# Four small edits at the joints of an attention kernel: value pieces at other steps, last sums in PSUM, half a norm on ScalarE

## The chip, the cores and the metric

The kernel runs on one core of a Trainium2 chip. The metric is the device time of one execution, in microseconds; a comparison takes the median of several runs. A core has five engines, each with its own queue of instructions, executed in order: PE (TensorE, matrix products, which it writes to the eight banks of PSUM), DVE (VectorE), ACT (ScalarE), POOL (GpSimd) and SP, which only starts transfers. They wait for each other by semaphores.

## What is computed

A chain of four blocks on x of shape 8 x 256 x 32 x 32, in float32: an attention block with an MLP, a deformable convolution, a binary convolution and another deformable convolution. The change lies in the first block, which is, cut to what matters:

```python
h = bn(x, g1, b1)                       # x as (8, 256, 1024), normed over batch and pixels
q, k, v = wq @ h + bq, wk @ h + bk, wv @ h + bv      # 16 heads; q, k of 16 rows, v of 64
a = softmax(q^T k * scale, axis=-1)     # 1024 x 1024 for each image and head
x = x + wp @ (a @ v) + bp
h = bn(x, g2, b2)
x = x + w2 @ relu6(w1 @ h + bb1) + bb2
```

## The kernel before, in words

**Tiling of attention.** The 8 images times 4 groups of 4 heads are 32 *groups* (b, g). A group has two *blocks* (b, g, h), h being a half (512) of the queries, so there are 64 blocks. A block goes over the 1024 keys in NT = 8 chunks of 128, one chunk to a *step*; there are 512 steps, 16 to a group. Of a step t:

- `exps` computes the scores of step t + 1 on PE (L453, four matmuls, keys on partitions) and their exponentials on ScalarE (L454). The maximum over the keys has been put into q as a row of its own, so that the matmul subtracts it.
- `attend` multiplies the exponentials of step t with the values on PE (L465), and sums exponentials over chunks by element: `esum`, L473 for the first two chunks, L475 for the others, on GpSimd; for the second pair of heads of the last block on VectorE.
- `score_max` finds the maxima for a later block (AHEAD = NT + 3 = 11 steps ahead): scores in bf16 pieces on PE (L408), maxima on VectorE (L412). `found(0)` to `found(3)` are four such pairs within a step. The first block has no bf16 pieces yet and takes `score_max_first` (L421 and L424), four pairs in each of the steps -11 to -4, which are the ramp; `enter_max` (L430 to L441) then turns the maxima and puts them into q with four small transfers.

**Order.** On PE, ScalarE, VectorE and GpSimd the order of instructions is the order of these calls, written out by hand (`manual_schedule`); SP's order is left to a scheduler. Work beside the core of the loop is entered by `plan(step, place, f, ...)`: in each step, the places 0, 1 and 2 run after `found(2)` and before `found(3)`.

**What is planned, for group n = (b, g) beginning at step t0:** the four pieces of the next group's values (`project_v`, eight matmuls and a copy by ScalarE to a piece, L391 and L395) at steps 0, 1, 2, and the fourth at 4 for even n and at 9 for odd n; the first group's own four pieces at -9, -7, -5 and -3; q and k of the next pair of groups (`project_qk`, L333) at 8, 9, 10 and 14 of even n, with their division into bf16 levels (`split`, L359 and L366 on VectorE, L364 on ScalarE) at 9 to 18; the transfers of the levels (`stack`, L374) and of q and k (`spread`, L380). A block's sums are taken by PE with a matrix of ones (`totals`, L486) three steps after its end, inverted and laid out by transfers, and its outputs scaled on GpSimd (L518) and projected (`add_projected`, L548) some steps later. The values of images after the first are normed on ScalarE (L317).

**The end.** The last block has a shorter way, `total_last` with reciprocals straight from PSUM (L526), and `scale_last` (L539, L540). Then follow `add_projected` (L548 on PE, L556 and L558 on VectorE), the batch norm's scale and shift (`batch_norm`, L207 to L219), and the MLP, which begins with `normed` (L749, two halves `t` of 128 channels) and `hidden` (L775). The MLP, the convolutions and the sampling between them are put in order by a planner with fixed costs (`Order`); the change doesn't touch its costs.

**Buffers that matter.** `bank()` in attention takes one of two PSUM banks (`pb`), shared by maxima, values, q and k, totals and projections; the scores have four (`sc`), the products with the values two. Exponentials have six tiles (`e`), two to a step. GpSimd and VectorE are the only engines that release them, except that the products on PE must be done too.

Of the kernel before, what the change touches and what calls it, by code (L numbers as in the profile page):

```python
# [12 lines left out]
AF = mybir.ActivationFunctionType  # L13
ALU = mybir.AluOpType
# [4 lines left out]
P = 128  # L19
# [4 lines left out]
NT = N // P  # L24
# [134 lines left out]
def conv_seq_kernel(ctx: ExitStack, tc: tile.TileContext, d: dict, out: bass.AP):  # L159
    nc = tc.nc  # L160
# [6 lines left out]
    x = const.tile([P, 2, B, N], F32, name="x")  # L167
# [12 lines left out]
    def col(name, i=0, n=1, p=P):  # L180
        o = COL[name] + i
        return vec[:p, o : o + n]
# [52 lines left out]
    wide = const.tile([P, 2, HID], F32, name="wide")  # L235
    with ExitStack() as s0:
# [20 lines left out]
        ones = w.tile([P, HD], F32, name="ones_a")  # L257
# [15 lines left out]
        for dst, name, eng in ((wq, "wqT", nc.sync), (wk, "wkT", nc.scalar)):  # L273
            padded = ep.tile([P, 2, HALF], F32, name="e")
            eng.dma_start(padded, d[name].rearrange("(t p) o -> p t o", p=P))
            for t in range(2):
                src = padded[:, t, :].rearrange("p (n r) -> p n r", r=32)[:, :, 0:KD]
# [3 lines left out]
        for dst, name, scale in ((bq4, "bq", 4.0), (bk, "bk", 1.0)):  # L281
            ps = ps_p.tile([P, 512], F32, name="pb")
            for c in range(4):
                nc.tensor.matmul(
                    ps[c % 2 * 64 : c % 2 * 64 + 64, c // 2 : c // 2 + 1], taken.rearrange("p n r -> p (n r)"), col(name, c),
                    start=True, stop=True,
# [8 lines left out]
        def bank():  # L295
            return ps_p.tile([P, 512], F32, name="pb")
# [11 lines left out]
        ys, vss, outs = {}, {}, {}  # L308

        def normed(b, t, h):  # L310
            if t == h == 0:
                ys[b] = yp.tile([P, 2, N], F32, name="y")
            cols = slice(h * HALF, (h + 1) * HALF)
            if b == 0:
                nc.vector.tensor_scalar(ys[b][:, t, cols], x[:, t, b, cols], s1[:, t : t + 1], t1[:, t : t + 1], ALU.mult, ALU.add)
            else:
                nc.scalar.activation(ys[b][:, t, cols], x[:, t, b, cols], AF.Identity, bias=t1[:, t : t + 1], scale=s1[:, t : t + 1])  # L317
# [34 lines left out]
        def split(b, g2, i, stage):  # L352

            which, h = QK[i]
            u, rest, lev = parts[i]

            eng = nc.gpsimd if (b, g2) == (0, 0) else nc.vector
            if stage == 0:
                eng.tensor_sub(rest, u, lev[0])  # L359
                return  # L360
            if lev[stage] is None:
                lev[stage] = lp.tile([P, HALF], BF16, name="lev")
            if stage == 1:
                nc.scalar.copy(lev[1], rest)  # L364
            else:
                eng.tensor_sub(lev[2], rest, lev[1])  # L366
            nc.sync.dma_start(lev_d[b, g2][which, stage, :, h * HALF : (h + 1) * HALF], lev[stage])
# [14 lines left out]
        def project_v(b, g, i):  # L382

            if i == 0:
                vss[b, g] = vp.tile([P, NT, 256], F32, name="v")
            ps = bank()
            for mt in (2 * i, 2 * i + 1):
                for t in range(2):
                    for c in range(2):
                        k0 = mt * P + c * 64  # L390
                        nc.tensor.matmul(  # L391
                            ps[c * 64 : (c + 1) * 64, (mt % 2) * 256 : (mt % 2 + 1) * 256], ys[b][:, t, k0 : k0 + 64],
                            wv[:, t, g * 256 : (g + 1) * 256], start=t == 0, stop=t == 1,
                        )
            nc.scalar.copy(vss[b, g][:, 2 * i : 2 * i + 2, :], ps.rearrange("p (m c) -> p m c", c=256))  # L395
# [47 lines left out]
        es = {}  # L443
# [12 lines left out]
        avs, sums = {}, {}  # L456

        def attend(m, kt, pair):
            b, g, h = m
            if kt == 0:  # L460
                avs[m, pair] = ps_v.tile([P, HALF], F32, name="av")
            av, e = avs[m, pair], es[m, kt, pair]
            for i in range(2):
                j = 2 * pair + i
                nc.tensor.matmul(  # L465
                    av[i * HD : (i + 1) * HD, :], vss[b, g][:, kt, j * HD : (j + 1) * HD], e[:, i, :],
                    start=kt == 0, stop=kt == NT - 1,
                )

            eng = nc.vector if m == blocks[-1] and pair else nc.gpsimd  # L470
            if kt == 1:
                sums[m, pair] = ap.tile([P, 2, HALF], F32, name="esum")
                eng.tensor_add(sums[m, pair], es.pop((m, 0, pair)), es.pop((m, 1, pair)))  # L473
            elif kt > 1:
                eng.tensor_add(sums[m, pair], sums[m, pair], es.pop((m, kt, pair)))  # L475
            if kt == NT - 1:
                outs[m, pair] = op.tile([P, HALF], F32, name="o")
                nc.scalar.copy(outs[m, pair], avs.pop((m, pair)))
# [3 lines left out]
        def totals(m):  # L482

            ps = bank()
            for j in range(4):
                nc.tensor.matmul(ps[32 * j : 32 * j + 32, :], ones[:, 0:32], sums[m, j // 2][:, j % 2, :], start=True, stop=True)  # L486
            return ps

        def total(m):
# [71 lines left out]
        blocks = [(b, g, h) for b, g in groups for h in range(2)]  # L561
# [7 lines left out]
        def plan(step, place, f, *args):  # L569
            work.setdefault((step, place), []).append(lambda: f(*args))  # L570

        for n, (b, g) in enumerate(groups):
            t0 = n * 2 * NT
            nxt = groups[n + 1] if n + 1 < len(groups) else None
            if nxt:
                for i in range(4):
                    plan(t0 + (0, 1, 2, 9 if n % 2 else 4)[i], 1, project_v, *nxt, i)
                    plan(t0 + 9 + i, 0, spread, *nxt, i)
                for pair in range(2):
                    for i in range(8):  # L580
                        plan(t0 + (1, 1, 2, 2, 2, 3, 3, 3)[i] + 4 * pair, 2, stack, *nxt, pair, i)
                if nxt == groups[-1]:
                    plan(t0 + 8, 2, nc.sync.dma_start, wide, d["w1T"].rearrange("(t p) o -> p t o", p=P))
            if g == 2 and b + 1 < B:
                for i in range(4):
                    plan(t0 + 5 + i // 2, i % 2, normed, b + 1, i // 2, i % 2)
            if n % 2 == 0 and n + 2 < len(groups):
                b_, g2 = groups[n + 2][0], groups[n + 2][1] // 2

                for i in range(4):  # L590
                    plan(t0 + (8, 9, 10, 14)[i], 1, project_qk, b_, g2, i)
                    at = t0 + (9, 11, 14, 17)[i]
                    plan(at, 0, split, b_, g2, i, 0)
                    plan(at, 2, split, b_, g2, i, 1)
                    plan(t0 + (10, 12, 16, 18)[i], 0, split, b_, g2, i, 2)
        for n, m in enumerate(blocks):
            b, g, h = m
# [43 lines left out]
        with tc.manual_schedule(engines={mybir.EngineType.PE, mybir.EngineType.Activation, mybir.EngineType.DVE, mybir.EngineType.Pool}):  # L641
            for t in range(2):
                for h in range(2):
                    normed(0, t, h)

            nc.scalar.dma_start(wv, d["wvT"].rearrange("(t p) o -> p t o", p=P))
            nc.gpsimd.dma_start(wp, d["wpT"].rearrange("(t p) o -> p t o", p=P))
            nc.gpsimd.dma_start(bv, d["bv"].rearrange("(t p) -> p t", p=P))
            for t in range(2):
                bias(t)  # L650
            for i in range(4):
                project_qk(0, 0, i)
                which, h = QK[i]
                for j in range(4):
                    dst = (qs, ks)[which][0][32 * j : 32 * j + KD, h * HALF : (h + 1) * HALF]
                    (nc.gpsimd if j % 2 else nc.sync).dma_start(dst, parts[i][0][j * KD : (j + 1) * KD, :])
                split(0, 0, i, 0)
            for i in range(4):
                plan(2 * i - 9, 1, project_v, 0, 0, i)
                split(0, 0, i, 1)  # L660
                split(0, 0, i, 2)
            for pair in range(2):
                for i in range(8):
                    stack(0, 0, pair, i, (nc.sync, nc.gpsimd))
            for t in range(-AHEAD, steps + 2 * NT):
                step(t)
            assert not work
# [11 lines left out]
    with ExitStack() as s1_:  # L679
# [34 lines left out]
        ones = w.tile([P, 1], F32, name="ones")  # L714
# [27 lines left out]
        ys, hids, pss = {}, {}, {}  # L742

        def normed(b, h):

            ys[b, h] = sb.tile([P, 2, HALF], F32, name="y")
            cols = slice(h * HALF, (h + 1) * HALF)
            for t in range(2):
                nc.vector.tensor_scalar(ys[b, h][:, t, :], x[:, t, b, cols], s2[:, t : t + 1], t2[:, t : t + 1], ALU.mult, ALU.add)  # L749

        def signs(t, i):

# [375 lines left out]
        b = B - 1  # L1128
# [21 lines left out]
        b = B - 1  # L1150
# [17 lines left out]
        with tc.manual_schedule(engines={mybir.EngineType.PE, mybir.EngineType.Activation, mybir.EngineType.DVE, mybir.EngineType.Pool}):  # L1168
            s2, t2 = batch_norm(1, col("g2", 0, 2), col("b2", 0, 2))
# [8 lines left out]
    with ExitStack() as s3_:  # L1178
# [61 lines left out]
        def bank3():  # L1240
# [17 lines left out]
            ps=2, pc=1, pd=1, pw=3, pa=1,  # L1258
# [374 lines left out]
        ps = bank3()  # L1633
# [247 lines left out]
```

## Time and profile before

| what | us |
|---|---|
| median of three runs (4491.49, 4504.40, 4504.44) | 4504.4 |
| the profiled execution | 4512.47 |
| its span, first to last instruction | 4510.7 |
| start to the first exponential's scores | 0 to 90.5 |
| attention from there to its last projection | 90.5 to 2661.5 |
| MLP, samples and binary convolution, first L775 to last L775 | 2667.2 to 3611.7 |

In a line of the timeline stand the start in us, the length in us (of a run of like instructions, where xN is over 1, from the first start to the last end), the engine, the line of the code, the operation, what it writes and reads, its sizes, and in brackets how long the engine had been idle before it and what ended that. A float32 matmul of the code is two in the trace, so the eight matmuls of a piece of values are x16. The windows give busy time by engine in a stretch of the span, with the mean granted clock of TensorE and the transfers.

### The profile page before, as it was taken

To read this page: it belongs to the slowest core of one execution; us is meant where nothing else is said; L and a number is where in the kernel's file an instruction comes from. 1 tells how busy PE (TensorE), PEld (TensorE's weight loads), DVE (VectorE), ACT (ScalarE), POOL (GpSimd) and SP (SyncE) were. 2 spreads that over 40 slices of the span, in tenths; PEclk is the share of its full clock that TensorE was granted. 3 is DMA by queue.
4 is the path that set the end of the run, shared out by engine and by line. 5 is a ranking of instruction groups with operands and counts; after the bars stand their busy time and mean duration, and the time that the engine had idled before them with its cause. 6 is when DMAs were issued, how large, how long until landed. Compare 5 with 4: busy or idle time off the path is not lost. (4 is left out here: it accounts for less than half of the span.)

```text
span 4510.7 us, 59867 instructions
## 1 busy us (share of the span) xinstructions
PE 4026.9 (89%) x20901; PEld 1530.0 (34%) x20901; DVE 2856.0 (63%) x4976; ACT 1875.1 (42%) x3366; POOL 3316.1 (74%) x2019
## 2 busy tenths in 40 slices
PE   6999999999999999999999998666767766899877
PEld 3333333333333333333333333222223322344332
DVE  5666666666666666666667653444445444688885
ACT  2555555555555555555555542211212111534331
POOL 3989988888888988898888954454454553078887
PEclk8999999999999999999999998888778878999978
DMA  5222221221222122122222112222232331100000
GB/s 164 67 63 56 63 75 57 63 69 57 61 72 63 56 64 74 56 61 70 59 62 71 48 45 69 78 80 79 76 96 68 89 110 60 40 10 15 15 15 24
DMA packets 224279, 284.12 MB, mean 63 GB/s; under 512 B 104400, under 2 KB 134624, under 8 KB 223712
## 3 DMA queue, kind: packets, MB, share of 16 engines
q1 hardware_dynamic: 193408, 196.49, 14.8%
q0 software_dynamic: 28720, 77.90, 5.8%
q10 hardware_dynamic: 1840, 5.81, 0.3%
q8 instruction: 168, 2.75, 0.3%
q14 instruction: 143, 1.17, 0.1%
HBM read 214.10 MB, written 64.34 MB: 62 GB/s over the span
## 5 line engine op out<-in xcount | busy, mean ns | idle before, releaser
L475 POOL TENSOR_TENSOR esum<-esum,e 128x1024 f32<-128x1024 f32 x762 | 1821.5, 2423 | 55.9 <-ACT e L454 55.4
L412 DVE TENSOR_REDUCE pm<-pb 128x1 f32<-128x512 f32 x2016 | 1372.9, 688 | 772.5 <-PE pb L408 769.7
L454 ACT ACTIVATE e<-sc 128x512 f32<-128x512 f32 x2048 | 1056.6, 603 | 601.0 <-PE sc L453 594.0
L465 PE MATMUL av<-e,v 128*64 128x512 f32 x4096 | 1048.5, 592 | 0.0
L930 POOL DMA_INDIRECT g<-table,idx x576 | 549.0, 953 | 583.4 <-DVE near_p L952 308.3
L408 PE MATMUL pb<-sk,sq 128*64 128x512 bf16 x4032 | 765.7, 386 | 17.8 <-DVE pm L412 17.1
L453 PE MATMUL sc<-q,k 32*128 32x512 f32 x4096 | 593.0, 639 | 0.0
L408 PEld LDWEIGHTS <-sq 128*64 128x64 bf16 x4032 | 247.2, 109 | 862.9 <-issue 849.1
L473 POOL TENSOR_TENSOR esum<-e 128x1024 f32<-128x1024 f32 x127 | 303.1, 2407 | 249.8 <-ACT e L454 246.5
L465 PEld LDWEIGHTS av<-e,v 128*64 128x64 f32 x4096 | 287.6, 137 | 232.1 <-issue 138.1
L788 PE MATMUL po<-hid,kept 128*128 128x512 f32 x512 | 260.1, 657 | 72.9 <-DVE x L792 56.4
L1500 POOL TENSOR_TENSOR part<-part,pr 128x512 f32<-128x512 f32 x212 | 275.8, 1301 | 55.4 <-DVE pr L1483 44.1
L1483 DVE TENSOR_TENSOR pr<-pw,v 128x512 f32<-128x512 f32 x394 | 253.8, 682 | 61.7 <-POOL part L1500 31.8
L1301 PE MATMUL pc<-xpad,kept 128*128 128x512 f32 x576 | 276.5, 604 | 11.2 <-DMA bom<-in_l_bom 7.9
L775 PE MATMUL pm<-y,wide 128*128 128x512 f32 x512 | 248.1, 632 | 17.0 <-ACT hid L780 11.3
L391 PE MATMUL pb<-wide,y 128*64 128x256 f32 x2048 | 248.6, 386 | 0.2 <-DVE pm L412 0.2
L453 PEld LDWEIGHTS sc<-q,k 32*128 32x128 f32 x4096 | 167.0, 183 | 231.0 <-issue 182.1
L548 PE MATMUL pb<-o,wp 128*64 128x512 f32 x1024 | 244.5, 598 | 0.4 <-DVE o L540 0.2
L780 ACT ACTIVATE hid<-pm,vec 128x512 f32<-128x512 f32 x128 | 86.8, 685 | 278.7 <-PE pm L775 142.5
L395 ACT COPY v<-pb 128x512 f32<-128x512 f32 x128 | 74.9, 585 | 296.1 <-PE pb L391 296.1
L952 DVE TENSOR_TENSOR near_p<-g,near_p 128x320 f32<-128x320 f32 (+1 forms) x384 | 177.3, 462 | 13.2
L391 PEld LDWEIGHTS pb<-wide,y 128*64 128x64 f32 x2048 | 143.5, 139 | 116.6 <-DVE pm L412 51.6
(266 smaller groups left out, 3927.2 us busy)
## 6 DMA issues: line engine op xcount, KB each, us to landing
sq<-lev_d SPq DMA_DIRECT2D x512, 64.0 KB
r<-inv_d SPq DMA_DIRECT2D x252, 128.0 KB
sk<-lev_d SPq DMA_DIRECT2D x496, 64.0 KB
lev_d<-lev SPq DMA_DIRECT2D x180, 128.0 KB
u_d<-u SPq DMA_DIRECT2D x60, 256.0 KB
g<-table,idx POOLq DMA_INDIRECT x576
out<-res SPq DMA_DIRECT2D x32, 256.0 KB
q<-u_d SPq DMA_DIRECT2D x124, 64.0 KB
```

The source lines that it names most:

```text
L391: nc.tensor.matmul(ps[c * 64 : (c + 1) * 64, (mt % 2) * 256 : (mt % 2 + 1) * 256], ys[b][:, t, k0 : k0 + 64], wv[:, t, g * 256 : (g + 1) * ...
L408: nc.tensor.matmul(ps[c * 64 : (c + 1) * 64, :], sq[pair][:, c, q0 : q0 + 64], sk[pair][:, c, kh * HALF : (kh + 1) * HALF], start=True, st ...
L412: nc.vector.tensor_reduce(maxima[m][:, pair, qt, kh : kh + 1], ps, AX.X, ALU.max)
L453: nc.tensor.matmul(ps, k[r, kt * P : (kt + 1) * P], q[r, h * HALF : (h + 1) * HALF], start=True, stop=True)
L454: nc.scalar.activation(es[m, kt, j // 2][:, j % 2, :], ps, AF.Exp)
L465: nc.tensor.matmul(av[i * HD : (i + 1) * HD, :], vss[b, g][:, kt, j * HD : (j + 1) * HD], e[:, i, :], start=kt == 0, stop=kt == NT - 1,)
L473: eng.tensor_add(sums[m, pair], es.pop((m, 0, pair)), es.pop((m, 1, pair)))
L475: eng.tensor_add(sums[m, pair], sums[m, pair], es.pop((m, kt, pair)))
L788: nc.tensor.matmul(pss["o", b, h, t], w2[:, j, t * P : (t + 1) * P], hids[b, h, j], start=j == 0, stop=j == 7)
L930: nc.gpsimd.indirect_dma_start(out=g[:, k, :], out_offset=None, in_=tables[b][:TR, :], in_offset=bass.IndirectOffsetOnAxis(ap=idxs[b][:, t ...
L1301: nc.tensor.matmul(S["c", b, h], wc[:, t, k, :], tap(xpads[t], k, H // 2, h * H // 2), start=t == k == 0, stop=t == 1 and k == 8,)
L1500: nc.gpsimd.tensor_add(S["part", b, h], S["part", b, h], S.pop(("pr", b, h, on_pool[n])))
```

## The change

Four things are edited.

1. `attend` doesn't add the exponentials of the last block's last two chunks; `totals` reads these tiles on PE instead and accumulates three sets of four matmuls in the bank, the sums last.
2. Steps of the values' pieces: the first group's pieces go from -9, -7, -5, -3 to one before the loop, then -3, -2 and 3; the fourth piece of the next group goes to step 12 in groups with g = 0 (it was at 4), and stays at 4 for g = 2 and at 9 for odd g.
3. The load of the MLP's first weights (`w1T`) is planned at step 13 of its group instead of 8.
4. In `normed` of the MLP, the second half of the first image's first pixels is computed by ScalarE instead of VectorE.

```diff
@@ attend @@
             eng = nc.vector if m == blocks[-1] and pair else nc.gpsimd
-            if kt == 1:
+            if m == blocks[-1] and kt > NT - 3:
+                pass
+            elif kt == 1:
                 sums[m, pair] = ap.tile([P, 2, HALF], F32, name="esum")
@@ totals @@
             ps = bank()
-            for j in range(4):
-                nc.tensor.matmul(ps[32 * j : 32 * j + 32, :], ones[:, 0:32], sums[m, j // 2][:, j % 2, :], start=True, stop=True)
+            late = (NT - 2, NT - 1) if m == blocks[-1] else ()
+            for i in range(len(late) + 1):
+                for j in range(4):
+                    src = es[m, late[i], j // 2] if i < len(late) else sums[m, j // 2]
+                    nc.tensor.matmul(
+                        ps[32 * j : 32 * j + 32, :], ones[:, 0:32], src[:, j % 2, :], start=i == 0, stop=i == len(late),
+                    )
             return ps
@@ the plan by groups @@
             if nxt:
+
+                late = {0: 12, 2: 4}.get(g, 9)
                 for i in range(4):
-                    plan(t0 + (0, 1, 2, 9 if n % 2 else 4)[i], 1, project_v, *nxt, i)
+                    plan(t0 + (0, 1, 2, late)[i], 1, project_v, *nxt, i)
                     plan(t0 + 9 + i, 0, spread, *nxt, i)
...
                 if nxt == groups[-1]:
-                    plan(t0 + 8, 2, nc.sync.dma_start, wide, d["w1T"].rearrange("(t p) o -> p t o", p=P))
+                    plan(t0 + 13, 2, nc.sync.dma_start, wide, d["w1T"].rearrange("(t p) o -> p t o", p=P))
@@ before the loop over steps @@
                 split(0, 0, i, 0)
+            project_v(0, 0, 0)
             for i in range(4):
-                plan(2 * i - 9, 1, project_v, 0, 0, i)
+                if i:
+                    plan((-3, -2, 3)[i - 1], 1, project_v, 0, 0, i)
                 split(0, 0, i, 1)
@@ normed of the MLP @@
             for t in range(2):
-                nc.vector.tensor_scalar(ys[b, h][:, t, :], x[:, t, b, cols], s2[:, t : t + 1], t2[:, t : t + 1], ALU.mult, ALU.add)
+                if b == h == 0 and t:
+
+                    nc.scalar.activation(ys[b, h][:, t, :], x[:, t, b, cols], AF.Identity, bias=t2[:, t : t + 1], scale=s2[:, t : t + 1])
+                else:
+                    nc.vector.tensor_scalar(ys[b, h][:, t, :], x[:, t, b, cols], s2[:, t : t + 1], t2[:, t : t + 1], ALU.mult, ALU.add)
```

## Prediction, written before the changed kernel ran

> **What bounds the kernel now.** I read the page first, then the windows over attention in stretches of 100 us, then the timelines of the four places that the diff touches: its ramp, the steps 11 to 13 of its groups, its end, and the first matmuls of the MLP.
>
> ```profile
> PE 4026.9 (89%) x20901; PEld 1530.0 (34%) x20901; DVE 2856.0 (63%) x4976; ACT 1875.1 (42%) x3366; POOL 3316.1 (74%) x2019
> ...
> PE   6999999999999999999999998666767766899877
> ```
>
> Attention is slices 2 to 23, and TensorE is full there: over 25 windows of 100 us (100 to 2600 us) PE is busy 2484.28 of 2500 us. So in attention a matmul that is moved costs the same elsewhere, and time comes only from where PE waits: about 16 us in steady state, the ramp, and the end. The ramp, by PE:
>
> ```profile
> 45.59 1.88 PE L333 MATMUL pb<-y,wq 128*64 128x512 f32 x8
> 48.95 0.69 PE L421 MATMUL sc<-k,q 16*128 16x512 f32 x1 [1.49 <-DMA k<-e]
> ...
> 55.91 3.63 PE L391 MATMUL pb<-wide,y 128*64 128x256 f32 x16
> ...
> 64.42 3.68 PE L391 MATMUL pb<-wide,y 128*64 128x256 f32 x16
> ...
> 74.09 3.68 PE L391 MATMUL pb<-wide,y 128*64 128x256 f32 x16
> ...
> 84.83 2.83 PE L391 MATMUL pb<-wide,y 128*64 128x256 f32 x16 [0.19 <-DVE pm L412]
> ...
> 90.48 1.14 PE L453 MATMUL sc<-q,k 32*128 32x512 f32 x8
> ```
>
> and by VectorE in the same stretch:
>
> ```profile
> 60.63 0.69 DVE L424 TENSOR_REDUCE pm<-pb 128x1 f32<-128x512 f32 x1 [3.33 <-PE sc L421]
> ...
> 70.14 0.69 DVE L424 TENSOR_REDUCE pm<-pb 128x1 f32<-128x512 f32 x1 [4.34 <-PE sc L421]
> ...
> 79.81 0.69 DVE L424 TENSOR_REDUCE pm<-pb 128x1 f32<-128x512 f32 x1 [4.33 <-PE sc L421]
> ```
>
> The ramp's chain is the 32 maxima of L424 on VectorE; each of the first three pieces of v (L391) stands between the score matmuls on PE and starves VectorE, 12.0 us in all. Steps 11 to 13 of a group with g = 0 (its ninth group):
>
> ```profile
> 792.94 2.73 DVE L359 TENSOR_TENSOR u<-u,lev 128x512 f32<-128x512 f32 x1
> ...
> 796.32 0.41 PE L408 MATMUL pb<-sk,sq 128*64 128x512 bf16 x2 [0.43 <-DVE pm L412]
> ...
> 798.44 2.29 DVE L366 TENSOR_TENSOR lev<-u,lev 128x512 bf16<-128x512 f32 x1
> ...
> 801.38 0.41 PE L408 MATMUL pb<-sk,sq 128*64 128x512 bf16 x2 [0.74 <-DVE pm L412]
> ```
>
> and the same two subtractions in the fifth group, where nothing waits:
>
> ```profile
> 471.57 0.70 DVE L359 TENSOR_TENSOR u<-u,lev 128x512 f32<-128x512 f32 x1
> ...
> 476.46 0.89 DVE L366 TENSOR_TENSOR lev<-u,lev 128x512 bf16<-128x512 f32 x1
> ```
>
> A subtraction that comes while GpSimd adds exponentials takes three times as long, the next maxima are late, and PE has no bank. By the starts of L453, steps 12 and 13 take 4.39 and 6.82 us in the ninth group (793.55, 797.94, 804.76), 3.77 and 5.52 in the fifth (472.18, 475.95, 481.47): 1.92 us lost. The end of attention and the MLP's first matmul:
>
> ```profile
> 2649.13 1.06 PE L486 MATMUL pb<-esum,ones_a 128*32 128x512 f32 x8 [2.52 <-POOL esum L475]
> 2650.26 3.39 DVE L526 RECIPROCAL r<-pb 128x128 f32<-128x128 f32 x4 [2.79 <-PE pb L486]
> ...
> 2662.84 3.98 POOL L719 MEMSET xb<- 128x2304 bf16 x2
> ...
> 2664.92 3.54 DVE L749 TENSOR_SCALAR y<-x,norm_s,norm_t 128x512 f32<-128x512 f32 x4
> 2667.24 1.19 PE L775 MATMUL pm<-y,wide 128*128 128x512 f32 x1 [5.75 <-DVE y L749]
> ```
>
> The first of the four L749 is the slow one: L749 has 528/536/2182 ns as least, median and most here, and its end (2664.92 + 2.18 = 2667.10) follows that of GpSimd's memsets (2666.82).
>
> **What the Trainium skill says.** SBUF — State Buffer, "Who interferes with whom": a VectorE instruction with two SBUF inputs and a GpSimd instruction that reads SBUF exclude each other, whichever comes first. The trace agrees: L359 0.70 against 2.73 us. TensorE: Matmul & The Clock Gate, "Part 1: The HAM clock gate": the array runs at half rate until it was busy for some 3.4 us. Here L391 takes 3.63 us in the ramp and 1.89 at 97.19, and the windows grant a clock of 0.50 from 65 to 85 us. ScalarE: Activation LUTs, "Table sets: the hidden batching unit": cheap functions such as identity are in every set. The trace agrees: the 28 Identity activations of L317 stand among exponentials and reload no table (0.83 us each).
>
> **The change, part by part.**
>
> *First piece of v (L663).* It moves from step -9 to PE's gap before the first scores (47.47 to 48.95, 1.49 us). Its weights were loaded last before 33 us (DMA share 1.04 in 20 to 30 us, 0.20 in 30 to 40), so it doesn't wait. At the full rate of L333 beside it, it takes 1.89 us: 0.4 more than the gap, so L424 starts at 50.5 instead of 50.11. Its copy (0.58 us) now stands ahead of L364 on ScalarE, about 1.2 us later; GpSimd's L366 behind that is only freed at 51.85. Nothing.
>
> *The other three.* With none left among the scores the 12.0 us go: 33.25 us of maxima (50.11 to 83.36) become 21.2, ending at 71.7. VectorE alone could do 32 x 0.60 = 19.3, so 69.8 to 72.5. From the last maximum to the first exponential's scores it was 7.1 us with one piece (83.36 to 90.48); now there are two. The second costs 1.9 us at full clock and 3.65 at half, plus 0.3 for a bank; the first may be half-rate throughout, 0 to 0.8. I take 2.2 + 0.4, since a piece at 84.83 brought the clock up within itself (2.83). So L453 starts at 71.7 + 7.1 + 2.6 = 81.4 instead of 90.48: -9.0. The rows of maxima land at the latest 4.1 us after VectorE's last transpose (86.36), about 79, and the first sq and sk are needed at 71, while their loads end at about 72 with the first pair's half ahead: no new wait. The last piece goes to step 3, where PE is full: a step with a piece takes 5.50, one without 3.77, so +1.73. Ramp: -7.3, of which I book **-7** (-8.5 to -4).
>
> *Fourth piece in g = 0 groups (8 of 32), step 4 to 12.* Step 4 falls from 5.50 to 3.77, step 12 gains the same; it pays where VectorE is late. I replay the ninth group: L408 at 797.39 stays, the piece runs from 797.65 to 799.5 in the bank of a maximum done at 797.46, then one L408, and L453 at 799.7; its ideal is 793.55 + 5.49 = 799.04. The next maxima need a bank freed at 801.33, and reach it at about 801.9: no wait. So 1.92 becomes 0.65: -1.27. The pair of waits (0.43 and 0.75) stands in the groups 8, 12, 16, 20, 24 and 28 counted from 0; group 0 has one of 0.44, group 4 none. 6 x 1.27 = **-7.6**. Bounds: 0 if the new order only shifts the waits, -11.5 if both subtractions go ahead of GpSimd (6 x 1.92). GpSimd falls no further behind: each block's first step has no sum, and it waits 217.8 us in 60 blocks there for exponentials.
>
> *Last block's sums.* Two additions less on GpSimd (3.1 us each there) and two on VectorE. PE is done at 2646.61 and need not wait 2.52 us; it runs 24 matmuls instead of 8. 8 take 1.06 and 16 more at the 0.107 of one following another 1.7: 2.77 us, done at 2649.4 instead of 2650.19. L518 comes some 3 us earlier too, but the reciprocals (3.39 us) set the bank behind it. **-0.8**, with L556's wait of 0.23 gone **-1** (-1.5 to 0).
>
> *Normed half on ScalarE.* PE's first matmul still waits for VectorE's half, the slow one; the second half was 0.5 us later and is covered by a first matmul of 1.19 us. ScalarE was idle for 6.84 us. **0** (-0.3 to +0.3).
>
> *w1T at step 13 instead of 8.* Its place in SP's queue is the same in both orders; only one pair of loads for the second group moves behind the four maxima rows. **0**.
>
> Sum: -7 - 7.6 - 1 = -15.6. Against the profiled execution (4512.47 us, span 4510.7): 4496.9. That execution is 8 us above the median of the three runs, 4504.4, and the saving doesn't scale, so 4504.4 - 15.6 = **4489 us**.
>
> **Rivals.**
> - *One of the two savings fails.* The stage's waits depend on 0.3 us (in the fifth group L359 came 0.02 us before GpSimd's next addition, in the ninth 0.27 after), and the ramp on the clock. For: both. Against: six groups repeat to 0.02 us. 4504.4 - 8 = 4496.
> - *More:* both subtractions go ahead in g = 0 groups, and the ramp takes its low end: -11.5 - 8.5 - 1 = 4483.
> - *Slower: the clock in the MLP and sampling stage.* Nine windows of 100 us from 2772 have a mean clock of about 0.81, so 38% of 900 us, 340 us, at half rate. The stage starts 15 us earlier against the throttle's windows and draws them anew. A half-rate microsecond under matmuls costs 0.5, so from 31 us more of it the gain is eaten; with 40 more it is +20 - 15.6: 4509. For: three runs of the unchanged kernel are 13 us apart. Against: PE is 62 to 76% busy there and mostly waits for samples, and it may as well fall shorter.
>
> **How the numbers follow.** Forecast 0.52 (own range 4482 to 4496), one saving only 0.28, more 0.10, slower 0.10. 0.3%, what a measurement of this kernel can tell from no change, is 13.5 us: below 4490.9 is faster, above 4517.9 slower. The forecast lies just beyond the line: 0.36 of its 0.52 count as faster; with the 0.10 of more, 0.46. Of the slower rival 0.06 passes 4517.9. The rest, 0.48, is no change that can be told. The range takes in the low end of more and most of the slower rival: 4477 to 4506.
>
> **What would show it.** Right: no VectorE gap over 1 us among L424, the first L453 near 81 us; no wait of 0.74 in step 13 of g = 0 groups while g = 2 groups keep theirs; L486 x24 without a wait for GpSimd; L775 still 2.3 us after L219. Wrong: L453 at 86 or later, steps 12 and 13 of g = 0 together over 11.7 us (11.02 is the ideal), or a changed length from the first L775 to the end.

## The result, and the profile after

| kernel, in one comparison | median us | lowest to highest | runs |
|---|---|---|---|
| before | 4498.14 | 4491.49 to 4505.83 | 15 |
| changed | 4487.77 | 4477.23 to 4498.48 | 15 |

The ratio is 0.9972 (95% interval 0.9963 to 0.9981), 12.6 us less (8.5 to 16.6), and 10.4 by the two medians; the sum had said 15.6. The predicted 4489 us are met to 1 us partly by luck: the kernel before ran 6 us lower in this comparison than in the three runs the sum began from, the medians' saving is 5 us smaller than the sum, and the two errors cancel. The test of the steps is therefore in the trace. First the page of the changed kernel:

```profile
PE 4016.8 (90%) x20917; PEld 1528.6 (34%) x20917; DVE 2849.6 (64%) x4973; ACT 1876.2 (42%) x3367; POOL 3309.2 (74%) x2017
...
PE   7999999999999999999999998666767757999877
```

TensorE issues 16 instructions more (the two added sets of four matmuls, two in the trace each), GpSimd and VectorE two and three less, and in attention (slices 1 to 23) only the first digit of PE's row changes. A few microseconds can't be seen on the page; they are seen in the timeline. Its ramp, on PE:

```profile
46.58 1.88 PE L333 MATMUL pb<-y,wq 128*64 128x512 f32 x8
48.29 1.89 PE L391 MATMUL pb<-wide,y 128*64 128x256 f32 x16
50.12 0.69 PE L421 MATMUL sc<-k,q 16*128 16x512 f32 x1
...
74.75 3.68 PE L391 MATMUL pb<-wide,y 128*64 128x256 f32 x16 [0.18 <-DVE pm L412]
...
80.90 1.95 PE L391 MATMUL pb<-wide,y 128*64 128x256 f32 x16 [0.19 <-DVE pm L412]
...
83.00 1.14 PE L453 MATMUL sc<-q,k 32*128 32x512 f32 x8
...
86.20 1.84 PE L453 MATMUL sc<-q,k 32*128 32x512 f32 x8
```

and on ScalarE, at its end:

```profile
82.90 0.58 ACT L395 COPY v<-pb 128x512 f32<-128x512 f32 x1 [3.83 <-PE pb L391]
83.50 1.28 ACT L454 ACT_TABLE_LOAD   x1
84.79 2.06 ACT L454 ACTIVATE e<-sc 128x512 f32<-128x512 f32 x4
```

The first piece of v fills the gap before the scores, none stands among them, two stand at the end. The first scores for exponentials (L453) begin at 83.00 instead of 90.48. But now ScalarE empties a piece of v at the very moment at which they begin, and its table load (the load of ScalarE's table of functions, ahead of the exponential) comes after that copy. Before, it ended 2.0 us ahead of the first exponentials:

```profile
88.32 1.28 ACT L454 ACT_TABLE_LOAD   x1
91.63 0.60 ACT L454 ACTIVATE e<-sc 128x512 f32<-128x512 f32 x1 [2.03 <-PE sc L453]
```

Steps 11 to 13 of the ninth group (L408 with its waits, the piece, and VectorE's two subtractions):

```profile
785.75 2.72 DVE L359 TENSOR_TENSOR u<-u,lev 128x512 f32<-128x512 f32 x1
...
789.13 0.41 PE L408 MATMUL pb<-sk,sq 128*64 128x512 bf16 x2 [0.43 <-DVE pm L412]
...
790.41 1.92 PE L391 MATMUL pb<-wide,y 128*64 128x256 f32 x16
791.25 2.29 DVE L366 TENSOR_TENSOR lev<-u,lev 128x512 bf16<-128x512 f32 x1
...
792.14 0.41 PE L408 MATMUL pb<-sk,sq 128*64 128x512 bf16 x2
...
793.55 0.41 PE L408 MATMUL pb<-sk,sq 128*64 128x512 bf16 x2
```

The subtractions are as slow as before. The wait of 0.43 stays, the wait of 0.74 is gone: PE has the piece to work on. The end:

```profile
2632.67 1.92 PE L491 MATMUL pb<-e,ones_a 128*32 128x512 f32 x16
2634.41 1.04 PE L491 MATMUL pb<-esum,ones_a 128*32 128x512 f32 x8
2635.52 3.39 DVE L533 RECIPROCAL r<-pb 128x128 f32<-128x128 f32 x4 [2.04 <-PE pb L491]
...
2650.17 0.81 ACT L762 ACTIVATE y<-x,norm_t,norm_s 128x512 f32<-128x512 f32 x1 [0.82 <-DVE norm_t L219]
2650.17 3.09 DVE L764 TENSOR_SCALAR y<-x,norm_s,norm_t 128x512 f32<-128x512 f32 x3
2652.50 10.33 PE L790 MATMUL pm<-y,wide 128*128 128x512 f32 x20 [5.75 <-DVE y L764]
```

(L477 was L475, L491 was L486, L533 was L526, L555 was L548, L563 was L556, L764 was L749, L790 was L775.) The totals no longer wait 2.5 us for GpSimd's sum. The MLP still waits for VectorE's half, 2.33 us after the batch norm, against 2.32 before.

So the MLP's first matmul comes at 2652.50 instead of 2667.24: 14.7 us earlier, of them 7.5 up to the first L453.

### The profile page after: what moved, and what is told of

The parts are those of the page before. It is cut to its first block, busy times and chain, and to the rows that moved or that the text cites. A ratio compares the mean times of both kernels' runs of the same rounds, so it can differ in the third digit from the quotient of the medians.

```text
span 4486.0 us, 59890 instructions
## 1 busy us (share of the span) xinstructions
PE 4016.8 (90%) x20917; PEld 1528.6 (34%) x20917; DVE 2849.6 (64%) x4973; ACT 1876.2 (42%) x3367; POOL 3309.2 (74%) x2017
## 4 chain that ended last, share of the span: by engine, by line
PE 74%; DVE 7%; another core or an unknown queue 7%; POOL 5%; issue 4%; ACT 1%; DMA 1%; SPq 0%; DVEq 0%; POOLq 0%; ACTq 0%
PE av L465 19%; PE sc L453 12%; PE pb L408 11%; PE pb L391 5%; PE pb L555 5%; PE pm L790 4%; PE pc L1316 3%; PE po L803 3%; PE pb L333 3%; POOL part L1515 2%; PE pc L1038 2%; DVE near_p L967 1%; PE pb L491 1%; PE pa L1507 1%
## 5 line engine op out<-in xcount | busy, mean ns | idle before, releaser
L477 POOL TENSOR_TENSOR esum<-esum,e 128x1024 f32<-128x1024 f32 x760 | 1814.7, 2421 | 49.2 <-ACT e L454 48.7
L945 POOL DMA_INDIRECT g<-table,idx x576 | 548.5, 952 | 565.0 <-DVE near_p L967 290.7
L408 PE MATMUL pb<-sk,sq 128*64 128x512 bf16 x4032 | 765.9, 386 | 12.7 <-DVE pm L412 12.1
L453 PE MATMUL sc<-q,k 32*128 32x512 f32 x4096 | 591.0, 639 | 0.0
L408 PEld LDWEIGHTS <-sq 128*64 128x64 bf16 x4032 | 246.2, 109 | 854.2 <-issue 840.8
L475 POOL TENSOR_TENSOR esum<-e 128x1024 f32<-128x1024 f32 x127 | 303.1, 2407 | 242.2 <-ACT e L454 242.2
L790 PE MATMUL pm<-y,wide 128*128 128x512 f32 x512 | 243.4, 622 | 14.5 <-ACT hid L795 8.8
L391 PE MATMUL pb<-wide,y 128*64 128x256 f32 x2048 | 244.3, 381 | 0.4 <-DVE pm L412 0.4
L555 PE MATMUL pb<-o,wp 128*64 128x512 f32 x1024 | 242.8, 594 | 1.9 <-DVE r L533 1.7
L453 PEld LDWEIGHTS sc<-q,k 32*128 32x128 f32 x4096 | 165.2, 183 | 231.1 <-issue 184.7
L971 DVE TENSOR_TENSOR samp<-samp,near_p 128x320 f32<-128x320 f32 (+1 forms) x384 | 174.0, 453 | 13.2
```

What stands on the lines that cost most here:

```text
L391: nc.tensor.matmul(ps[c * 64 : (c + 1) * 64, (mt % 2) * 256 : (mt % 2 + 1) * 256], ys[b][:, t, k0 : k0 + 64], wv[:, t, g * 256 : (g + 1) * ...
L408: nc.tensor.matmul(ps[c * 64 : (c + 1) * 64, :], sq[pair][:, c, q0 : q0 + 64], sk[pair][:, c, kh * HALF : (kh + 1) * HALF], start=True, st ...
L453: nc.tensor.matmul(ps, k[r, kt * P : (kt + 1) * P], q[r, h * HALF : (h + 1) * HALF], start=True, stop=True)
L555: nc.tensor.matmul(ps[c * 64 : (c + 1) * 64, :], wp[:, 2 * g + i, o0 : o0 + 64], outs[(b, g, h), i], start=i == 0, stop=i == 1,)
L790: nc.tensor.matmul(ps, w1[:, t, i * P : (i + 1) * P], ys[b, h][:, t, :], start=t == 0, stop=t == 1)
L945: nc.gpsimd.indirect_dma_start(out=g[:, k, :], out_offset=None, in_=tables[b][:TR, :], in_offset=bass.IndirectOffsetOnAxis(ap=idxs[b][:, t ...
```

## The experiments

The experiments ran on two chips, 1 to 8 on one and 9 to 12 on the other; the kernel before takes some 4160 us on the first and 4510 on the second. No chip is on record for the first comparison; its times (4498 us) and its mean clock (0.94, where the first chip has 0.975) fit the second. The ratios are to the kernel before on the same chip. Times of the whole are too blunt for parts of 1 to 8 us, so the reading is two landmarks of each trace: the first L453, and the stretch from it to the MLP's first matmul. Runs 1 to 4, 8 and 9 edit the kernel before; 5, 6, 7, 10 and 11 edit the changed one.

| kernel | first L453 | from it to the MLP | MLP's first matmul | ratio to before (95%) |
|---|---|---|---|---|
| before | 90.48 | 2576.8 | 2667.24 | |
| before again (run 8 below) | 89.27 | 2577.3 | 2666.56 | |
| changed | 83.00 | 2569.5 | 2652.50 | 0.9972 (0.9963 to 0.9981) |
| changed again (12) | 82.63 | 2569.3 | 2651.94 | 0.9975 (0.9965 to 0.9985) |
| 1 ramp alone | 82.16 | 2580.1 | 2662.21 | 0.9988 (0.9982 to 0.9995) |
| 2 g = 0 pieces alone | 90.15 | 2568.5 | 2658.69 | 0.9978 (0.9969 to 0.9988) |
| 3 last sums alone | 89.57 | 2576.2 | 2665.78 | one run |
| 4 norm alone | 90.35 | 2578.0 | 2668.35 | one run |
| 5 o's projection at 12 | 82.26 | 2565.9 | 2648.11 | 0.9964 (0.9950 to 0.9977) |
| 6 one piece less in the ramp | 81.09 | 2571.2 | 2652.30 | one run |
| 7 subtractions earlier | 82.64 | 2568.5 | 2651.11 | 0.9971 (0.9960 to 0.9983) |
| 9 GpSimd idle at the subtractions | 89.41 | 2566.7 | 2656.06 | one run |
| 10 q/k piece at 11 or 12 | 84.05 | 2555.4 | 2639.48 | 0.9943 (0.9924 to 0.9961) |
| 11 two q/k pieces | 82.64 | 2558.9 | 2641.51 | 0.9949 (0.9932 to 0.9966) |

Runs of the same ramp differ by about 1 us in the first landmark (by 1.9 with run 10), those of the same steps by 0.5 in the second (by 1.2 with run 4, whose totals ran at a reduced rate, as in run 1 below).

**1 to 4: each edit alone, on the kernel before.** The ramp:

```diff
+            project_v(0, 0, 0)
             for i in range(4):
-                plan(2 * i - 9, 1, project_v, 0, 0, i)
+                if i:
+                    plan((-3, -2, 3)[i - 1], 1, project_v, 0, 0, i)
```

> The kernel before with only the first group's value pieces moved (one before the loop, then steps -3, -2 and 3). My theory: VectorE's gaps of 3.33, 4.34 and 4.33 us among the 32 maxima go, the first L453 starts near 83 us (90.48 before), and the first matmul of the MLP comes 6 to 7.5 us earlier than before's 2667.24; in the steps 12 and 13 of g = 0 groups PE still waits 0.43 and 0.74 us. Rival 'all of it is the steady state': the MLP's start moves by under 2 us.

The first L453 is 7.1 to 8.3 us earlier than in the two runs of the kernel before, and 2.8 to 3.3 us are given back after it, so 4.4 to 5.0 are left. Of those given back, 1.73 are the piece in step 3 (3.77 to 5.50), as booked. 0.65 are step 0, which takes 6.2 instead of 5.55 in this run and in every other with the new ramp: the exponentials begin 1.80 us after the first L453 instead of 1.16, behind the table load shown above (read from the traces; no run moved the load). The rest is at the end, and is no work of this edit: there the totals, still behind their wait for GpSimd, ran at a reduced rate, 1.71 us for what took 1.06.

```profile
2643.47 1.71 PE L486 MATMUL pb<-esum,ones_a 128*32 128x512 f32 x8 [2.50 <-POOL esum L475]
```

The pieces of the g = 0 groups:

```diff
+                late = {0: 12, 2: 4}.get(g, 9)
                 for i in range(4):
-                    plan(t0 + (0, 1, 2, 9 if n % 2 else 4)[i], 1, project_v, *nxt, i)
+                    plan(t0 + (0, 1, 2, late)[i], 1, project_v, *nxt, i)
```

> The kernel before with only the fourth piece of g = 0 groups at step 12 instead of 4. My theory: the wait of 0.74 us in step 13 goes in the groups 8, 12, 16, 20, 24 and 28, the one of 0.43 stays, the subtractions still take 2.7 and 2.3 us, g = 2 groups are as before, and the MLP starts 7 to 8 us earlier. Rival 'the waits only shift': PE waits as long elsewhere in those groups and the MLP starts within 2 us of before.

8.2 to 8.8 us go between the landmarks. The waits say where: of the groups 8, 12, ... 28 each keeps 0.43 and loses the second wait, and the single wait of group 0 (0.44) goes too. Steps 12 and 13 of such a group together take 11.63 us instead of 11.21, with the piece of 1.73 in them: 1.3 gained. 6 x 1.3 and 0.6 for group 0 are 8.4.

The last sums and the norm (their diffs are parts 1 and 4 of the change):

> The kernel before with only the last block's last exponentials summed on PE. My theory: the MLP starts 0.5 to 1.3 us earlier (PE saves 2.52 us of waiting and gives back 1.7 in matmuls; the reciprocals behind it are as long). Rival 'it takes the whole wait': 2.5 us earlier, or more with GpSimd's scaling out of the way.

> The kernel before with only the second half of the MLP's first normed pixels on ScalarE. My theory: the MLP's first matmul starts as before, within 0.2 us, 2.3 us after the last step of the norm's shift (L219), since the half that stays on VectorE is the slow one. Rival 'the half was on the path': 0.5 us or more earlier against L219.

The sums bring 0.6 to 1.1 us between the landmarks. From the start of the projection ahead of the totals (L548) to the MLP it is 21.64 us with them, 21.65 in the changed kernel, 22.52 in the kernel before: 0.9. The norm brings nothing: from the batch norm's end to the first matmul 2.35 us (that the matmul itself comes 1.1 us later than before lies ahead of the norm: the totals took 1.67 us instead of 1.06). So the parts measured alone, about -5, -8.5, -0.9 and 0, make -14.4, and the whole change 14.7: to within the noise of the landmarks they add up. The weights' load, part 3, was not run alone.

**9 (and 8): why are the subtractions slow?** In the kernel before, GpSimd's additions that lie beside them are left out:

```diff
-            if kt == 1:
+            if g == 0 and h == 1 and kt in (3, 4, 5):
+                pass
+            elif kt == 1:
```

> The kernel before, without GpSimd's additions of the exponentials of chunks 3 to 5 in the second block of each g = 0 group (those chunks are left out of the sums there, so the weights are normed by too little). These are the additions that GpSimd works on while the subtractions of the split i = 1 come at steps 11 and 12; the other groups keep theirs. (The run before this one that was to leave them out named chunks 11 to 13, which a block of 8 chunks doesn't have, and was the kernel before unchanged.) Theory (the subtractions wait for GpSimd's additions): in g = 0 groups L359 takes 0.7 and L366 0.9 us or less, the waits of 0.43 and 0.74 go, and the MLP's first matmul comes at 2667 - 6 x 1.92 = 2655.5; in g = 2 groups 2.7 and 2.3 us stay. Rival (they are slow for another reason): unchanged at 2.3 us and more in both kinds of group, the first matmul within 2 us of 2667.

VectorE's and GpSimd's timelines in the ninth group (L520 was L518):

```profile
791.63 0.68 DVE L359 TENSOR_TENSOR u<-u,lev 128x512 f32<-128x512 f32 x1
...
796.52 0.68 DVE L366 TENSOR_TENSOR lev<-u,lev 128x512 bf16<-128x512 f32 x1
```

```profile
783.91 2.51 POOL L520 TENSOR_TENSOR o<-r,o 128x512 f32<-128x512 f32 x2
798.40 4.66 POOL L477 TENSOR_TENSOR esum<-esum,e 128x1024 f32<-128x1024 f32 x2 [11.99 <-ACT e L454]
```

With GpSimd idle (11.99 us) the subtractions take 0.68 instead of 2.73 and 2.29, both waits are gone in every g = 0 group, and the MLP's first matmul is at 2656.06, where 2655.5 was expected. The g = 2 groups, whose additions are kept, keep 2.7 and 2.3 us and both waits, but for one group, whose waits come earlier (0.49 and 0.90, and then 0.44), as they do in runs 4, 6, 8 and 10. So the slow subtractions belong to GpSimd's additions. The Trainium skill, SBUF — State Buffer, "Who interferes with whom", says that a VectorE instruction with two SBUF inputs contends with a GpSimd instruction that reads SBUF; the run agrees, by taking the other party away. It doesn't vary which of the two comes first. The run made first for this named chunks that a block doesn't have, and so was the kernel before once more; it is the second reference in the table:

> The kernel before, without GpSimd's additions of the exponentials of key tiles 11 to 13 in the first block of each g = 0 group (those tiles are left out of the sums there, so the weights are normed by too little). GpSimd is then idle or ahead when the two subtractions of the split i = 1 come. Theory (they take 2.73 and 2.29 us[...]): L359 and L366 take about 0.7 and 0.9 us in all of these groups, the waits of 0.43 and 0.74 go, and the MLP's first matmul comes at about 2667.2 - 6 x 1.92 = 2655.7. Rival (they are slow for another reason, such as ScalarE or DMA traffic): they stay at 2.3 us or more, and the MLP starts within 2 us of 2667.2.

**7: the subtractions a step earlier**, in the changed kernel:

```diff
-                    at = t0 + (9, 11, 14, 17)[i]
+                    at = t0 + (9, 10, 14, 17)[i]
-                    plan(t0 + (10, 12, 16, 18)[i], 0, split, b_, g2, i, 2)
+                    plan(t0 + (10, 11, 16, 18)[i], 0, split, b_, g2, i, 2)
```

> The changed kernel, with the first and the last stage of the second split (i = 1) one step earlier: the subtraction L359 at step 10 instead of 11, L366 at step 11 instead of 12. Steps 10 and 11 hold a projection piece each, so PE is behind there and VectorE has slack; the fourth value piece stays at step 12 in g = 0 groups and at step 4 in g = 2 groups. Theory (PE waits because a late subtraction falls into a step without a projection): the waits of 0.43 and 0.75 go in both kinds of group. In g = 0 groups 0.65 us each remain, in g = 2 groups 1.92, so 6 x 0.65 + 8 x 1.9 = about -19 us at the MLP's first matmul against 2652.5 in the changed kernel. Rival (a subtraction of 2.7 us outlasts even a step of 5.5): the waits only move to steps 10 and 11, and the MLP starts within 3 us of 2652.5, or later.

The rival holds: the first landmark apart, only 1 us is gained. VectorE and PE in a g = 2 group:

```profile
943.28 0.81 DVE L366 TENSOR_TENSOR lev<-u,lev 128x512 bf16<-128x512 f32 x1
944.02 2.84 DVE L359 TENSOR_TENSOR u<-u,lev 128x512 f32<-128x512 f32 x1
```

```profile
947.51 0.41 PE L408 MATMUL pb<-sk,sq 128*64 128x512 bf16 x2 [0.68 <-DVE pm L412]
```

A full step isn't enough cover by itself: step 10 now has two subtractions in a row, and each group that makes q and k has one wait in step 11 in place of the later ones, of 0.68 in all but two (0.96 and 1.32).

**5 and 10: what can cover a slow subtraction?** In the changed kernel, g = 2 groups have no piece in step 12. Run 5 puts the projection of o there, whose result VectorE adds to x:

```diff
-                at = (7, 10) if m == blocks[-1] else (9, 10) if m == blocks[-2] else (13, 15)
+                at = (7, 10) if m == blocks[-1] else (9, 10) if m == blocks[-2] else (12, 15) if (g, h) == (1, 1) else (13, 15)
```

> The changed kernel, with the first projection of o of the blocks g = 1, h = 1 at step 12 of the next group instead of step 13, so that the groups with g = 2 have PE work in step 12 as those with g = 0 now have. Theory (any filler of 1 us or more of PE work in step 12 covers the wait of 0.75 in the next step): it goes in the g = 2 groups; each gains up to 1.27 us as the g = 0 groups did; about -8 us at the MLP's first matmul (-10 to -4, since this piece is 1.9 us of matmuls but needs the scaled o, which may come late), the first wait of 0.43 stays. Rival (only a piece that takes its bank at the right moment does it): 0.75 stays or becomes a wait for o, within 2 us of 2652.5.

```profile
953.33 0.68 DVE L563 TENSOR_TENSOR x<-pb,x 128x512 f32<-128x512 f32 x1
...
954.06 0.41 PE L408 MATMUL pb<-sk,sq 128*64 128x512 bf16 x2 [0.56 <-DVE x L563]
```

It gains about 3.5 us of the 8 between the landmarks (4.4 at the MLP's first matmul, just inside the expected 4 to 10): the second wait for the maxima is gone, and one of 0.56 for L563 has come, since the bank of this piece is emptied by the engine that is late. Neither reading, as it was put, held: between them lies a wait of another kind. Run 10 takes a piece that ScalarE empties, the third of q and k:

```diff
-                    plan(t0 + (8, 9, 10, 14)[i], 1, project_qk, b_, g2, i)
+                    plan(t0 + ((8, 9, 11, 14) if g == 0 else (8, 9, 12, 14))[i], 1, project_qk, b_, g2, i)
```

> The changed kernel, with the third piece of q and k (L340's projection, emptied by ScalarE) at step 11 instead of 10 in g = 0 groups and at step 12 instead of 10 in g = 2 groups. Theory (a PE piece whose bank ScalarE empties, put into the lean step of the late subtraction, covers the wait; the projection of o does not because VectorE empties its bank): in g = 0 groups the wait of 0.43 goes (-0.65 each), in g = 2 groups the 0.75 goes and the 0.43 stays (-1.27 each); step 10 becomes lean and has only the subtraction of 0.81, so no new wait there; -12 us at the MLP's first matmul against the changed kernel (-14 to -8), 2640.5. Rival (VectorE has too much in steps 9 to 13 together, wherever the pieces stand): a new wait at step 10 of 0.4 or more, and the MLP's first matmul within 4 us of 2652.5.

The eleventh group, one with g = 2, on PE, VectorE and ScalarE:

```profile
945.52 2.13 DVE L359 TENSOR_TENSOR u<-u,lev 128x512 f32<-128x512 f32 x1
...
948.30 0.41 PE L408 MATMUL pb<-sk,sq 128*64 128x512 bf16 x2
...
949.59 1.91 PE L333 MATMUL pb<-y,wk 128*64 128x512 f32 x8
...
950.43 2.30 DVE L366 TENSOR_TENSOR lev<-u,lev 128x512 bf16<-128x512 f32 x1
951.31 0.41 PE L408 MATMUL pb<-sk,sq 128*64 128x512 bf16 x2
951.60 0.69 ACT L346 ACTIVATE u<-pb,bk 128x512 f32<-128x512 f32 x1 [1.34 <-PE pb L333]
```

No line of L408 has a wait of 0.4 or more any longer, but for one group (0.49 and 0.90 at 618 to 624), the same as in run 9; the 0.43 of the g = 2 groups went as well, which wasn't expected: L359 now comes earlier against GpSimd's additions and takes 2.13 us instead of 2.72. It does so in the g = 0 groups too (2.12 us), so there this run can't tell the cover of the piece at step 11 from the faster subtraction. For the second wait, in g = 2 groups, it can: L366 is as slow as before (2.30) and nothing waits. Between the landmarks 14 us are gained on the changed kernel (12 expected), and on the same chip the run's interval lies below that of the changed kernel (0.9924 to 0.9961 against 0.9965 to 0.9985). This version beats both kernels: 4481.77 us, beside 4499.38 for the changed one and 4510.03 for the one before.

**11: both lean steps filled**, with the fourth piece moved from 14 to 12 in g = 2 groups, (8, 9, 11, 12):

> As the run with the third piece at 11 and 12, but in g = 2 groups the third piece at step 11 and the fourth at step 12 instead of 14, so that both lean steps of those groups are filled and steps 10 and 14 are lean. Theory: both waits go in g = 2 groups (-1.92 each) and the 0.43 in g = 0 groups (-0.65 each): about -17 us against the changed kernel, the MLP's first matmul at 2635. Rival (VectorE is late at step 14 as well, where the third subtraction stands): a new wait of 0.4 or more at step 14 or 15 of g = 2 groups, so no better than the other run.

The waits of steps 12 and 13 go, and in five g = 2 groups one of 0.60 to 0.62 comes after step 14, in step 15 (and one of 1.38, in step 13, in the third group), as the rival said; its stretch is 3.4 us longer than that of run 10.

**6: one piece less in the ramp**, at (-2, 3, 4):

> The changed kernel, with the first group's pieces of v at steps -2, 3 and 4 instead of -3, -2 and 3: one piece fewer between the last maxima and the first exponentials, one more in a full step. Theory (the ramp ends with two pieces at reduced clock in a row, 3.68 and 1.95 us): the first L453 comes 3 to 4 us earlier than 83.0 unless the rows of maxima hold it at about 80.5; step 4 grows by 1.73, so -1 us at the MLP's first matmul (-2.5 to +1). Rival (the half clock lasts into the one piece that is left): the first L453 is only 1.9 us earlier or less, and nothing or up to +1.5 us is left of it.

```profile
77.94 3.01 PE L391 MATMUL pb<-wide,y 128*64 128x256 f32 x16 [0.19 <-DVE pm L412]
81.09 1.14 PE L453 MATMUL sc<-q,k 32*128 32x512 f32 x8
```

The rival holds: without the first of the two, the other is the slow one (3.01 instead of 1.95 us). The first L453 gains 1.2 to 1.9 us and step 4 gives 1.73 back. A piece that had taken 3.68 us in the changed kernel is gone, and a third to a half of it is saved, because the piece that is left is no longer run at the full rate that the other had brought (granted clock 0.63 while it runs, 1.00 in the changed kernel).

**12: the changed kernel once more**, on the chip that is slower in the MLP:

> The changed kernel itself, measured beside the three others of this call. Theory (the parts add up, -5.0 from the ramp, -8.5 from the g = 0 groups, -1 from the last sums, and what else differed between the two first traces lies in the MLP and sampling stage's own spread): the MLP's first matmul at 2652.5 +-1 as before, and the whole about 14 us below the kernel before, ratio 0.9966 (0.9958 to 0.9975). Rival (a part of the gain is given back behind the MLP's start): the first matmul at 2652.5 again, but the whole less than 9 us below the kernel before.

The trace repeats to 0.6 us. The whole is 10.7 us below the kernel before by the medians (11.3 by the ratio, 6.8 to 15.8), so between the two readings; the interval holds both, and the run decides neither.

## Why the prediction was right, by its steps

- **What bounds the kernel.** Right: time came from three places where PE waits, and nowhere else in attention.
- **First piece.** Right: it takes 1.89 us and waits for no weights. The first maximum was put at 50.5 and comes at 51.28, in two other ramps of this kind (12 and 1) at 50.95 and 50.50. The difference lies ahead of the piece: in all three the maximum comes 4.70 us after PE's last L333 begins, and that is at 46.58, 46.25 and 45.80, against 45.59 in the trace of before.
- **The other three.** The first L453 was put at 81.4, and came at 83.0, 82.6 and 82.2. The stretch from the last maximum to it was put at 9.7 us and is 9.7, 9.5 and 9.2. The term that was mis-sized is the 21.2 us of maxima: they take 22.0 to 22.5, since the score matmuls on PE, at a granted clock of 0.50, still end small waits of VectorE among them:

```profile
71.39 0.69 DVE L424 TENSOR_REDUCE pm<-pb 128x1 f32<-128x512 f32 x1 [0.37 <-PE sc L421]
```

  From 60 to 72 us PE is busy 12.00 us by the profile, in all three of these traces, and the clock stays at 0.50: the prediction's statement that some 3.4 us of being busy bring the full rate does not hold here. L391 at 74.75, which took 3.68 us, was followed by one of 1.95.

  The table load lost its cover: the prediction counted the copies and not this load, which ended 2.0 us ahead of the first exponentials in the trace of before. So the -7 was about -5 by its parts: -7.1 to -8.3, then +1.73 (booked) and +0.65 (not). The Trainium skill, ScalarE: Activation LUTs, "Table sets: the hidden batching unit", puts such a load at about 2.7 us; the same page, "What ACT_TABLE_LOAD costs", splits that into 1283 ns for the load and the rest for a drain. The 1.28 us agree with the first; no drain is seen here, since the load follows the copy and the exponentials follow the load within 0.02 us, which decides. Of the 1.28 us, 0.65 came through.
- **g = 0 groups.** Right: -7.6 predicted, -8.2 to -8.8 measured, which makes up for a part of what the ramp lacks; the replay of the ninth group (no second wait, the first stays) came out as written. The single wait of group 0 had been seen and not counted. That both waits belong to GpSimd's additions is now shown, not only argued.
- **Last sums.** Right: -1 predicted, -0.9 measured. The 24 matmuls take 2.78 us, 2.77 had been worked out.
- **Norm and w1T.** Nothing was predicted. For the norm that is shown; w1T was not run alone, and the sum of the other parts leaves little room for it. The MLP's first matmul still waits for y, not for the weights.
- **The sum.** -15.6 predicted, -14.7 and -15.3 at the MLP's first matmul in the two traces of the changed kernel. Over the whole it is -12.6 and -11.3 by the ratios. The intervals hold 14.7 too, so whether 2 to 4 us are lost behind the MLP's start is open; the traces show no loss there. From the MLP's first matmul to the end of the span, on the slower chip, they have 1843.4 and 1844.3 us (before and run 9) and 1833.5, 1836.7, 1840.0 and 1832.6 (changed, 12, 10 and 11). The prediction had named a changed length of this stretch as a sign of being wrong, and it is 7 to 10 us shorter in the two traces of the changed kernel. But whole executions of the changed kernel on that chip lie 19 us apart (4488.87 to 4507.59), while the start of the MLP repeats to 0.6 us in its two traces, so a trace or two can't tell it from chance.
- **The slower rival, the clock in the MLP.** It didn't happen. Over the nine windows from 2767 us the mean clock is 0.81 before and 0.83 and 0.82 in the two traces of the changed kernel. One saving only (4496) is ruled out by the runs of single parts.

## What to carry to other kernels

A stall on the critical engine can be cured without touching its cause, by moving work of that engine into it; in these runs it mattered which engine releases the buffer of the moved work. A piece emptied by ScalarE, which is busy for 42% of the span, covered the second wait of a group (runs 2 and 10); a piece emptied by the late VectorE changed it into another (run 5). Such a move also shifts the work that caused the stall, as L359 in run 10, so both have to be looked at. When work is taken from a ramp at reduced clock, count what then runs cold in its place, and what first-time cost (here a table load) had been hidden by it.

## What was not expected of the hardware

The same kernel, before, takes some 4160 us on one chip and 4510 on the other. Attention is alike (the MLP begins at 2666.6 and 2667.2); most of the difference is in the stage of the MLP and the sampling: from the MLP's first to its last first-layer matmul it is 945 us in the first trace of before and 655 in the second (run 8). The waits there, in the stretch 2750 to 3250 us, of the changed kernel on the slower chip:

```profile
POOL g L945 <- DVE near_p L967: 166.8, 12, 25.4
DVE x L807 <- remote: 85.7, 6, 18.9
ACT hid L795 <- remote: 78.7, 9, 23.2
```

and of run 7 on the other:

```profile
ACT near_p L954 <- DVE samp L971: 116.4, 38, 9.0
...
POOL g L945 <- DVE near_p L967: 5.8, 19, 0.3
```

(The columns are the us in total, how often, and the longest.) On the slower chip engines stand up to 23 us at a time for something that the profile can't name ("remote"), and GpSimd, which issues the gathers (L945), waits for VectorE up to 25 us at a time; in the trace of run 7 on the other chip there is no "remote" line. What it is stays open.

The clock is less sure than one trace shows. After the same wait of 2.5 us for GpSimd, the eight totals matmuls took 1.06 us in the two traces of before and in run 2, and 1.71, 1.67 and 1.93 in runs 1, 4 and 9, where the granted clock was about 0.6, 0.6 and 0.5 meanwhile, instead of 1.00. The skill's TensorE: Matmul & The Clock Gate, "Part 1: The HAM clock gate", has the activity window free-running, and of some 3.4 us; that a shorter wait lets the clock fall in some executions and not in others would fit, but no run here varied it.
